# A four-layer graph network: PSUM handed out by single banks, rows turned by transposing transfers, parts of elu and beta added by transfers, and a new order of the work

## The chip, the cores and the metric

The kernel runs on one core of one Trainium2 chip. A core has five instruction queues that run side by side: TensorE (PE), VectorE (DVE), ScalarE (ACT), GpSimd (POOL) and SyncE (SP). Each takes its instructions strictly in the order in which the program lists them, and waits at one whose data or buffer is not there. Matmul results go to PSUM, which has eight banks of 512 float32 columns; the other tiles lie in SBUF. The metric is the time of one execution on the device in microseconds; less is better.

## The reference

There are eight graphs of 2048 nodes with 128 features in float32, and one 2048 x 2048 matrix of edges for all of them. Each of four layers normalizes the rows (layer norm, then the larger of the value and 0), works on the result `h`, and adds what comes out to `x`:

```
layers 0, 1, 3:  Wh = h W;  e = leaky_relu(Wh a1 + (Wh a2)^T);  no edge: -9e15
                 x += f(softmax(e) Wh)        f: elu, nothing, elu
layer 3:         Wh is normalized first, and added to softmax(e) Wh before elu
layer 2:         four heads of 32 features:  e = leaky_relu(h h^T);  no edge: -inf
                 x += softmax(e) h
```

## The kernel before, in words

**Units.** A graph's layer is a unit: 24 graph units (class `Gat`, layers 0, 1 and 3) and 8 of heads (class `Heads`, layer 2). Within a graph its layers follow one another; the eight graphs are independent, and the kernel mixes units of different graphs.

**Building a unit.** VectorE takes the moments of the rows (L471), POOL the power -1/2 (L113), ScalarE makes the rows `h` in four quarters of 512 nodes (L538). A quarter is turned, so that the features lie on the partitions: four 128 x 128 transposes on TensorE into PSUM (L569), then a copy to SBUF. For a graph unit ScalarE copies it to `h_t` (L590), TensorE multiplies it with the weights (L599), and ScalarE makes from the products the values `y` and the exponentials of the scores (L637 to L652). For heads the copy (L964) rounds it to `hi`, VectorE takes the rest `lo` (L968), and SP stores both parts and `h` to DRAM (L973, L952), from where they are loaded again head by head: `s` (L987), `m` (L995), `v` (L1000).

**Tokens.** A graph unit's attention goes by two halves of 1024 target nodes and 16 blocks of source nodes; a half and a block is a token, 768 in all. VectorE makes the 128 x 1024 weights `zg` with one instruction (L767), and TensorE adds eight 128 x 129 products to three PSUM banks (L776; in float32 each shows as two matmuls). After 16 tokens VectorE divides by the sums into `oa` (L808, L809). Layer 1 adds `oa` to `x` by an accumulating transfer that POOL issues (L845). Layers 0 and 3 apply elu, with -1 taken beforehand: ScalarE makes exp of `oa` into `oe` and the larger of `oa` and 0 (L815), VectorE adds the smaller of `oe` and 1 to `x` (L839), and a transfer adds `oa`. Layer 3 first adds the rows by a transfer (L893), multiplies by gamma (L832) and adds beta (L834) on VectorE. There is one `oa` and one `oe`. The last graph's layer 3 and a few places listed in `DIRECT` use VectorE instead of transfers.

**Beats.** A head and a block of 128 source nodes is a beat, 512 in all. TensorE makes 128 x 2048 scores with four matmuls in two pairs (L1063), ScalarE takes exp of each pair's 1024 columns (L1070), VectorE masks all 2048 columns with one instruction that also adds them up (L1076), and TensorE multiplies with the values in 32-column tiles (L1085). After a head's 16 beats the result is copied, turned, divided and added to `x` by a transfer (L1094 to L1110).

**PSUM.** Banks 1 to 3 hold a token half's sums and bank 0 a head's result. Banks 4 to 7 are two pairs, taken by whatever else needs PSUM: scores, transposes, projections, small sums.

**Who sets the order.** `Plan` (L178) is a planner that runs when the program is built. Each piece of work is added with its engine, a cost, a due time, what it needs, and the buffers it takes and frees (L191); `run` (L201) then starts, step by step, on the engine that can start first, the piece of lowest due time among those ready within a small window. The order found is each queue's order in the program. The slots of each buffer stand in L262. Due times come from three tables: `TOKENS` (start of each half), `BEATS` (start and step of each head) and `LEADS` (how long before its start a unit is begun).

## Time and profile before

| what | value |
|---|---|
| runs | 2681.71 us median of 3 (2679.57 to 2682.79) |
| profiled execution | 2679.22 us, its span 2677.4 us, granted TensorE clock 0.992 |
| first and last score matmul | 280.6 us, 2542.6 us |
| TensorE idle time | 78.8 us in all, 34.4 of it between 268 and 2546 us |
| tokens on VectorE (L767) | 768 of 1.279 us |
| masks on VectorE (L1076) | 512 of 2.285 us |
| exps on ScalarE (L1070) | 1024 of 1.111 us |
| VectorE adds of 128 x 1024 (L834, L839) | 16 of 1.220 us, 32 of 1.221 us |
| accumulating transfers of 512 KB (L845, L893) | 40 and 14; POOL busy 0.9 us each; 4.9 and 4.6 us to landing |
| bytes moved | 196.49 MB, 73 GB/s on average |

A line of the profile's groups names the source line, engine and operation, what is written and read, and how often; behind the bar stand the busy time in us, the mean of one in ns, and the idle time of the engine just before them, with what ended most of it. PEld is TensorE's loading of weights, which runs beside matmuls. Overlapping instructions count once in a busy time, so that a mean can be larger than busy time over count.

### The profile page before, as it was taken

The numbers are of one execution on the slowest core, as the hardware profiler recorded it, in microseconds if no ns is written. First come the engines' busy times: TensorE is split into PE (matmuls) and PEld (weight loads), VectorE is DVE, ScalarE is ACT, GpSimd is POOL, SyncE is SP. The second block draws the span as 40 slices with busy tenths as digits, with TensorE's granted clock in tenths as the row PEclk, the third lists the DMA queues.
The fourth block names the chain that finished last, engine by engine and source line by source line (L and its number), as shares of the span: only waits on it lengthen the run. The fifth ranks groups of instructions, "written<-read, shape, count | busy, mean of one in ns | idle before, by whom it ended". The sixth has DMA issues, their size and how long they took to land. (4 is left out here: it accounts for less than half of the span.)

```text
span 2677.4 us, 49161 instructions
## 1 busy us (share of the span) xinstructions
PE 2598.6 (97%) x20104; PEld 2041.9 (76%) x20104; DVE 2482.8 (93%) x3304; ACT 1719.8 (64%) x2777; POOL 279.8 (10%) x143
## 2 busy tenths in 40 slices
PE   7999999999999999999999999999999799999997
PEld 7899877687777786888777768787766478676587
DVE  8867989989999999999999999999999799999987
ACT  2526555767776677647766778674676866778751
POOL 1200000010100110011110101011101110010020
PEclk9999999999999999999999999999999999999999
DMA  9002423144344332362424434424315321542121
GB/s 319 17 9 63 97 52 67 10 94 103 81 88 99 62 62 56 60 123 56 86 50 87 79 78 87 82 48 88 72 42 93 64 40 56 115 68 64 33 52 34
DMA packets 216875, 196.49 MB, mean 73 GB/s; under 512 B 142896, under 2 KB 178176, under 8 KB 210496
## 3 DMA queue, kind: packets, MB, share of 16 engines
q1 hardware_dynamic: 144112, 156.46, 22.5%
q0 software_dynamic: 72112, 36.73, 12.0%
q8 instruction: 160, 2.62, 0.4%
q14 instruction: 75, 0.61, 0.1%
q10 hardware_dynamic: 416, 0.07, 0.0%
HBM read 123.03 MB, written 33.73 MB: 59 GB/s over the span
## 5 line engine op out<-in xcount | busy, mean ns | idle before, releaser
L776 PEld LDWEIGHTS ps<-y,zg 128*128 128x128 f32 x12288 | 1449.5, 192 | 66.1 <-DVE zg L767 17.0
L776 PE MATMUL ps<-y,zg 128*128 128x129 f32 x12288 | 1472.5, 276 | 13.6 <-DVE zg L767 10.0
L1070 ACT ACTIVATE z<-ps,shift 128x1024 f32<-128x1024 f32 x1024 | 1091.1, 1111 | 525.4 <-PE ps L1063 513.4
L1076 DVE SCALAR_TENSOR_TENSOR z<-z,edge 128x2048 f32<-128x2048 f32 x512 | 1160.0, 2285 | 26.9 <-ACT z L1070 26.6
L767 DVE SCALAR_TENSOR_TENSOR zg<-r,cr,edge 128x1024 f32<-128x1024 f32 x768 | 969.4, 1279 | 113.6 <-PE ps L776 101.9
L1063 PE MATMUL ps<-m,s 128*128 128x512 f32 x2048 | 627.0, 421 | 21.8 <-ACT z L1070 10.9
L1063 PEld LDWEIGHTS ps<-m,s 128*128 128x128 f32 x2048 | 341.0, 190 | 268.4 <-ACT z L1070 147.8
L1085 PE MATMUL ps<-z,v 128*32 128x512 f32 x4096 | 499.7, 601 | 1.5 <-DVE z L1076 1.3
L1085 PEld LDWEIGHTS ps<-z,v 128*32 128x32 f32 x4096 | 103.9, 109 | 223.8 <-issue 175.0
L538 ACT ACTIVATE h<-x,nmrx,rstdx 128x128 f32<-128x128 f32 x512 | 207.0, 485 | 48.5 <-DVE nmrx L118 36.0
L113 POOL TENSOR_TENSOR rstdx<-varx,neg_half 128x16 f32<-128x16 f32 x31 | 122.1, 3940 | 458.0 <-DVE varx L108 444.6
L1110 POOL DMA_DIRECT2D x<-o x31 | 65.8, 2124 | 747.9 <-DVE o L1105 608.2
L845 POOL DMA_DIRECT2D x<-oa x40 | 36.9, 922 | 748.5 <-ACT z L1070 199.5
L599 PE MATMUL ps<-rhs,h_t 128*128 128x130 f32 x768 | 104.9, 283 | 4.6 <-DVE h_t L590 2.7
L599 PEld LDWEIGHTS ps<-rhs,h_t 128*128 128x128 f32 x768 | 95.4, 195 | 12.6 <-ACT h_t L590 7.1
L471 DVE BATCH_NORM_STATS2 st<-x 128x6 f32<-128x128 f32 x496 | 100.4, 278 | 3.3 <-DMA x<-oa 3.3
L569 PE MATMUL ps<-ident,h 128*128 128x128 f32 x512 | 79.7, 280 | 4.2 <-ACT z L1070 1.7
L809 DVE TENSOR_TENSOR oa<-ps,rs 128x384 f32<-128x384 f32 x144 | 73.9, 513 | 5.1
L815 ACT ACTIVATE oe<-oa 128x1024 f32<-128x1024 f32 x32 | 33.9, 1058 | 69.0 <-DVE oa L834 55.3
L590 ACT COPY h_t<-ps 128x512 f32<-128x512 f32 x92 | 52.6, 585 | 33.2 <-PE ps L569 33.1
L569 PEld LDWEIGHTS ps<-ident,h 128*128 128x128 f32 x512 | 60.9, 143 | 16.6 <-ACT h L538 4.3
L637 ACT ACTIVATE y<-ps,y 128x128 f32<-128x128 f32 x240 | 68.6, 369 | 0.0
(129 smaller groups left out, 833.8 us busy)
## 6 DMA issues: line engine op xcount, KB each, us to landing
s<-halves SPq DMA_DIRECT2D x256, 128.0 KB, 2.8
m<-halves SPq DMA_DIRECT2D x64, 512.0 KB, 6.8
r<-row SPq DMA_DIRECT2D x42, 512.0 KB, 3.9
x<-oa POOLq DMA_DIRECT2D x40, 512.0 KB, 4.9
raw<-in_adj_dram SPq DMA_DIRECT2D x16, 1024.0 KB, 15.5
values<-h SPq DMA_DIRECT2D x32, 256.0 KB, 2.3
halves<-hi SPq DMA_DIRECT2D x128, 64.0 KB, 1.7
halves<-lo SPq DMA_DIRECT2D x128, 64.0 KB, 1.7
```

The source lines that it names most:

```text
L113: nc.gpsimd.tensor_tensor(out=rstd, in0=v, in1=neg_half, op=OP.pow)
L471: nc.vector.bn_stats(out=key["st"][:, n, :], in_=rows()[:, n, :])
L538: nc.scalar.activation(self.h[q][:, k, :], X[self.b][:, n, :], AF.Relu, scale=key["rstd"][:, n:n + 1], bias=key["nmr"][:, n:n + 1])
L569: nc.tensor.transpose(pk[:, k, :], self.h[q][:, k, :], ident)
L599: nc.tensor.matmul(pv[:, k, :C + 2], lhsT=self.h_t[q][:, k * P:(k + 1) * P], rhs=rhs, start=True, stop=True)
L767: nc.vector.scalar_tensor_tensor(z, self.r[half], self.cr[:, 0, jb:jb + 1], edge[:, jb, half * HN:(half + 1) * HN], op0=OP.max, op1=OP.mult)
L776: nc.tensor.matmul(ps[:, self.banks(half, place)[i // 3], k * CE:(k + 1) * CE], lhsT=z[:, i * P:(i + 1) * P], rhs=self.y[:, jb, :], start= ...
L809: nc.vector.tensor_mul(key["a"][:, i0:i1, :], pv[:, :, :C], r[:, i0:i1, None].to_broadcast([P, i1 - i0, C]))
L1063: nc.tensor.matmul(ps[:, lo + c, :], lhsT=self.S[h, jb // HB][:, at:at + P], rhs=self.M[h][:, (c2 * 2 + c) * 512:(c2 * 2 + c + 1) * 512], ...
L1070: nc.scalar.activation(self.z[s][:, c2 * HN:(c2 + 1) * HN], ps[:, lo:lo + 2, :].rearrange("p b t -> p (b t)"), AF.Exp, bias=shift)
L1076: nc.vector.scalar_tensor_tensor(self.z[s], self.z[s], 1.0, edge[:, jb, :], op0=OP.mult, op1=OP.mult, accum_out=self.den[:, h, jb:jb + 1])
L1085: nc.tensor.matmul(ps[c * HD:(c + 1) * HD, 0, :], lhsT=self.V[h][:, jb, :], rhs=z[:, c * 512:(c + 1) * 512], start=jb == 0, stop=jb == NB - 1,
```

## The change

*Single banks.* The planner hands out banks 4 to 7 one by one. A work item can take two of them (the second place for a half's sums). Each score matmul and each exp of 512 columns is an item of its own; projections, the values made of them, and the exponentials that TensorE spreads over all partitions for three units are split by bank.

*Rows turned by transfers.* In all units but the seven in `ON_PE`, ScalarE copies a quarter's low and high 16 bits into two planes `pl`, SP issues one transposing transfer of `pl` to `tr`, and ScalarE merges the planes into `h_t`. `pl` and `tr` have one buffer each; `h` has two instead of three. For heads, `hi` and `lo` are then made from `h_t` in SBUF, and `lo` overwrites it.

*Parts of elu and beta by transfers.* ScalarE makes the larger of -`oa` and 0, then exp of its negative, which is the smaller of exp(`oa`) and 1, so that a transfer can add it to `x`; three ScalarE instructions instead of two. In graphs 0 to 6, beta is added to `oa` by a transfer from a source that is repeated. The last graph and `DIRECT` keep VectorE's add of elu.

*Order.* The costs and delays that the planner reckons with are others; token halves follow a list `HALVES` at a fixed distance, heads start at `PLACES`, and `LEADS` is new. 

```diff
-        plan = Plan(dict(pair=(4, 6), sums=(0,), more=(1,), low=0, z=5, zg=3, r=2, h=3, h_t=2, hi=1, lo=1,
+        plan = Plan(dict(bank=(4, 5, 6, 7), sums=(0,), more=(1,), low=0, z=5, zg=3, r=2, h=2, h_t=2, pl=1, tr=1, hi=1,
...
+    PLANES, TURNED, ON_PE = 1, 1, ((0, 0), (1, 0), (0, 1), (0, 2), (7, 1), (7, 2), (7, 3))
...
+            def turned_by_transfer(self, q, part, made, kept=None):
+                key = {}
+                def split(op):
+                    key["pl"] = big.tile([P, 2, 4 * P], U16, tag="pl", name="pl", bufs=PLANES)
+                    nc.scalar.copy(key["pl"], self.h[q].rearrange("p k c -> p (k c)").bitcast(U16).rearrange(
+                        "p (n two) -> p two n", two=2))
+                def move(op):
+                    key["tr"] = big.tile([P, 8, P], U16, tag="tr", name="tr", bufs=TURNED)
+                    nc.sync.dma_start_transpose(out=key["tr"], in_=key["pl"].rearrange("p two n -> p (two n)"))
+                def merge(op):
+                    self.h_t[q] = quarter("h_t")
+                    nc.scalar.copy(self.h_t[q].bitcast(U16).rearrange("p (n two) -> p two n", two=2),
+                                   key["tr"].rearrange("p (two k) n -> p two (k n)", two=2))
+                parted = add("ACT", SPLIT_US, self.due(part), split, made[1:], takes=["pl"], frees=[] if kept else [("h", made[0])])
+                moved = add("SP", MOVE_US, self.due(part), move, [parted, kept], takes=["tr"],
+                            frees=[("pl", parted)] + [("h", made[0])] * (kept is not None),
+                            lag=MOVE_LAG_US)
+                return add("ACT", MERGE_US, self.due(part), merge, [moved], takes=["h_t"], frees=[("tr", moved)])
...
-                    turn = self.transposes(q, part, made[q], ["h_t"])
+                    by_pe = (self.b, layer) in ON_PE
+                    turn = self.transposes(q, part, made[q], ["h_t"]) if by_pe else None
...
+                        copied = turn = self.turned_by_transfer(q, part, made[q])
...
+                def below(op):
+                    key["e"] = key.get("e") or big.tile([P, HB, C], F32, tag="oe", name="oe", bufs=1)
+                    nc.scalar.activation(key["e"], key["a"], AF.Relu, scale=-1.0)
+                def grown(op):
+                    nc.scalar.activation(key["e"], key["e"], AF.Exp, scale=-1.0)
...
-                    e = e_taker = add("ACT", 0.95, due + 6, lambda op: whole(op, "e", AF.Exp), [last], takes=["oe"])
+                    e_taker = add("ACT", 0.95, due + 6, below, [last], takes=["oe"])
+                    e = add("ACT", 0.95, due + 7, grown, [e_taker])
...
+                        if k == 2 and b != B - 1:
+                            last = add("POOL", PLUS_US, due + 6 + 4 * k, lambda op: nc.gpsimd.dma_start(
+                                out=key["a"], in_=beta2_sb[:, None, :].to_broadcast([P, HB, C]), accum_op=OP.add),
+                                [last], lag=PLUS_LAG_US)
...
-                e = add("DVE", 1.14, late, elu_e, [e], frees=[("oe", e_taker)])
+                if (b, layer) in DIRECT or b == B - 1:
+                    e = add("DVE", 1.14, late, elu_e, [e], frees=[("oe", e_taker)])
+                else:
+                    e = add("POOL", PLUS_US, late, lambda op: nc.gpsimd.dma_start(
+                        out=xs(), in_=key["e"], accum_op=OP.add), [e], frees=[("oe", e_taker)], lag=PLUS_LAG_US)
...
+                        nc.scalar.copy(self.h_t[q, 0], rows_t(q, turn, by_pe))
...
+                        self.h_t[q, 1] = (quarter("h_t") if by_pe else self.h_t[q]).bitcast(F32R)
+                        nc.vector.tensor_sub(self.h_t[q, 1], rows_t(q, turn, by_pe), self.h_t[q, 0].bitcast(F32))
...
-                        for c2 in range(2):
-                            score = add("PE", 0.463, due - EARLY["score"] + c2, lambda op, s=s, c2=c2: self.scores(op, s, c2),
-                                        [score, ops[jb // HB], ops[2]], takes=["pair"] + ["z"] * (c2 == 0))
+                        for c in range(4):
+                            score = add("PE", SCORE_US, due - EARLY["score"] + 0.5 * c, lambda op, s=s, c=c: self.scores(op, s, c),
+                                        [score, ops[jb // HB], ops[2]], takes=["bank"] + ["z"] * (c == 0), lag=0.28)
...
+            def exp(self, op, s, c, bank):
+                if c == 0:
                     self.z[s] = big.tile([P, N], F32, tag="z", name="z", bufs=5)
+                nc.scalar.activation(self.z[s][:, c * 512:(c + 1) * 512], ps[:, bank, :], AF.Exp, bias=shift)
...
+        HALVES = (
+            (1, 0, 0), (1, 0, 1), (0, 1, 0), (0, 1, 1), (2, 0, 0), (2, 0, 1), (1, 1, 0), (1, 1, 1),
...
+        PLACES = (
+            374.047, 498.948, 515.464, 607.589, 669.983, 722.264, 807.407, 892.766, 873.536, 927.774,
...
```

## The prediction

> **What bounds the kernel now.** First the totals of the busy time, then the costliest groups of instructions.
>
> ```profile
> PE 2598.6 (97%) x20104; PEld 2041.9 (76%) x20104; DVE 2482.8 (93%) x3304; ACT 1719.8 (64%) x2777; POOL 279.8 (10%) x143
> ...
> L1070 ACT ACTIVATE z<-ps,shift 128x1024 f32<-128x1024 f32 x1024 | 1091.1, 1111 | 525.4 <-PE ps L1063 513.4
> L1076 DVE SCALAR_TENSOR_TENSOR z<-z,edge 128x2048 f32<-128x2048 f32 x512 | 1160.0, 2285 | 26.9 <-ACT z L1070 26.6
> L767 DVE SCALAR_TENSOR_TENSOR zg<-r,cr,edge 128x1024 f32<-128x1024 f32 x768 | 969.4, 1279 | 113.6 <-PE ps L776 101.9
> L569 PE MATMUL ps<-ident,h 128*128 128x128 f32 x512 | 79.7, 280 | 4.2 <-ACT z L1070 1.7
> L590 ACT COPY h_t<-ps 128x512 f32<-128x512 f32 x92 | 52.6, 585 | 33.2 <-PE ps L569 33.1
> ```
>
> TensorE is idle for 78.8 of 2677.4 us. ScalarE stands 513.4 us waiting for scores and VectorE 101.9 us for room that TensorE frees: both wait for TensorE. A busy TensorE need not be at its pace, so next I read the order in time of the weight loads, where starts follow one another if nothing is waited for.
>
> ```profile
> 1265.74 1.98 PEld L776 LDWEIGHTS ps<-y,zg 128*128 128x128 f32 x16
> 1267.63 0.47 PEld L569 LDWEIGHTS ps<-ident,h 128*128 128x128 f32 x4
> 1268.07 0.30 PEld L1063 LDWEIGHTS ps<-m,s 128*128 128x128 f32 x2
> 1268.42 3.77 PEld L776 LDWEIGHTS ps<-y,zg 128*128 128x128 f32 x32
> 1272.11 0.47 PEld L569 LDWEIGHTS ps<-ident,h 128*128 128x128 f32 x4
> 1272.55 0.30 PEld L1063 LDWEIGHTS ps<-m,s 128*128 128x128 f32 x2
> ```
>
> No waits stand here. Start to start, a token (16 loads, L776) after scores takes 1.89 us (1265.74 to 1267.63); two in a row take 3.69, so the second 1.79 or so. A quarter's four transposes (L569) take 0.44, both times. So removing them moves all that follows up by 0.44.
>
> Third, three stretches: from the start to the first scores, the middle in which heads and tokens are mixed, and the last tokens.
>
> ```profile
> 0.00:268.00 268.00, 244.77 (x2067) 234.57 (x2068) 202.97 (x357) 111.94 (x325) 32.30 (x25) 0.97 0.31 102
> 268.00:2546.00 2278.00, 2243.57 (x17072) 1699.55 (x17071) 2173.04 (x2793) 1561.97 (x2345) 233.41 (x111) 1.00 0.36 72
> 2546.00:2677.40 131.40, 110.22 (x970) 107.77 (x968) 106.83 (x155) 45.88 (x108) 14.13 (x8) 0.96 0.21 44
> ```
>
> Columns: window and length, then busy us of PE, PEld, DVE, ACT, POOL, clock, DMA share, GB/s. In the middle TensorE is 98.5% busy, VectorE 95.4%, ScalarE 69%: TensorE bounds, VectorE is close behind. Of the middle's 34.4 us without TensorE, 14.8 lie in one place:
>
> ```profile
> 2077.00:2144.00 67.00, 52.16 (x316) 29.27 (x319) 48.17 (x64) 54.08 (x105) 7.92 (x3) 0.92 0.33 63
> ```
>
> There ScalarE makes a unit's rows while the exps wait behind them in its order. The list of waits over the span (us in total, times, longest) has what follows from that:
>
> ```profile
> DVE z L1076 <- ACT z L1070: 26.6, 19, 16.9
> ...
> PE ps L1063 <- ACT z L1070: 10.9, 12, 3.3
> ```
>
> The longest wait of the first line, 16.9 us, stands in that window: VectorE has no exp to mask. So ScalarE's order can cost time even at 64%. The last line is TensorE's wait for a score bank that ScalarE has not emptied.
>
> **The change, part by part.** *Transposes.* 25 of 32 units (all but the seven in ON_PE) turn rows by transfer: 100 quarters. TensorE loses 100 x 0.44 = 44.0 us, on the path. Added per quarter: a split (128x1024 two-byte elements) and a merge on ScalarE, one transfer on SP. A graph unit's quarter loses a copy of 0.585. The nearest row of ScalarE for the split is the copy of 128x1024 floats, 1.007 us; I take 1.0 each, with ends 0.585 (half the bytes, L590) and 2.0 (128x2048, L442). ScalarE: 100 x 2.0 - 76 x 0.585 = +156 us (73 to 356). It is hidden as long as the exps behind it aren't late: ScalarE now stands 513 us waiting for scores.
>
> *The transfer's landing* is shown nowhere in this trace. Nearest rows, both 256 KB:
>
> ```profile
> values<-h SPq DMA_DIRECT2D x32, 256.0 KB, 2.3
> x<-o POOLq DMA_DIRECT2D x31, 256.0 KB, 7.8
> ```
>
> The first moves whole rows, the second adds in pieces of 128 bytes. I take 4, nearer the first, since the source rows are whole. A merge that ScalarE reaches before the landing blocks all exps queued behind it. In the changed program's order I summed ScalarE's own work between each split and its merge, with durations from the rows above and exps at 0.535: 2.1 to 20 us, median 6.4. Standing at the merges, over all 100, is then at most 0.2 us at a landing of 2.3, 11 at 4, 48 at 6, 149 at 7.8. I take 11, which the 513 us absorb: 0 on the path. SP carries 100 more issues; it stands before loads of s for 718.8 us over 46 waits (38.7 at most), so a transfer queued behind such a load starts late by that; the order interleaves them, and my 11 doesn't hold it: the upper end does. With one buffer each for pl and tr a unit's four quarters take at least 4 x (1.0 + 4 + 1.0) = 24 us, 39 at a landing of 7.8; that is hidden where a unit is begun early, and where one is not (the unit built from 2085 to 2116 took 31) up to some 10 us are late: rival (c). h has two buffers instead of three, but gives one back at the split or the transfer; the lo part is subtracted from SBUF instead of PSUM (0.685, taken as the same).
>
> By the Trainium skill's page "VectorE: DVE Perf Modes" (Rules for kernel authors, with The three transpose paths) TensorE should turn 128x128 blocks where PSUM will do; it has 1309 ns per block by transfer, and the eight two-byte blocks of a quarter would land after 10.5 us, an estimate. Then the standing would be 377 us and the change a loss if a seventh of it reached TensorE. The row of 256 KB above, 2.3 us, speaks for less, and no row here shows a transposing transfer.
>
> A second rule speaks against my bound: the skill's start page, "Trainium Kernel Development and Optimization" (Best Practices), judges TensorE by the share of its weight loads, not by its busy time. That is 76% here, and by it the 44 us would buy little. The starts 0.44 us apart with no wait between say otherwise.
>
> *Single banks.* Each score matmul takes its own bank and each exp has 512 columns: 2048 exps at 0.585 less the 0.05 by which neighbours overlap (1.111 against a start distance of 1.06) make 1096 against 1091: +5 us of ScalarE; without the overlap 1198, +107. A bank comes free after half the time, so I take the 10.9 us wait of TensorE as gone (0 to 34.4, the middle's idle time). Counted in both programs, changes between scores and tokens rise from 664 to 691; a token after scores starts its successor 0.10 later than one after a token, so +2.7 us. Projections go from one product of 8 loads to two of 4: same loads.
>
> *elu and beta.* VectorE loses 26 of L839 (1.221) and 14 of L834 (1.220): 48.8 us. ScalarE gains 32 x 1.058 = 34. POOL issues 40 more adds at 0.9 = 36 us, and the one that adds a waits for the landing of the one that adds e (4.9). Queued behind on POOL are powers (3.9 each) and gathers; VectorE waited only 5.2 us for powers. The single oa of a layer-3 half is held about 29 us instead of 19, of a layer-0 half 17 instead of 11; a half takes at least 16 x 1.79 = 28.6 us of TensorE, 55 on average, so the next divide is not late. Were it late, VectorE and the sums' three banks would stand, at most about 10 us per half. Value 0 on the path, as VectorE is not the pace.
>
> *Order.* In the changed program 127 tokens stand before the first score instead of 105, 56 after the last score in both. The front grows by 22 x 1.79 = 39.4 us and the middle shrinks by as much. VectorE in the middle then needs 2173.0 - 22 x 1.26 - 48.8 = 2096 of 2278.0 - 39.4 - 44.0 + 2.7 - 10.9 = 2186 us, 95.9% as against 95.4%: its relief is used up by the order, TensorE stays ahead. ScalarE in the middle: 1562 + 156 + 34 + 5 = 1757, 80%. Other stalls I leave as they are: a new order has other ones.
>
> Sum against the profiled execution (span 2677.4 + 1.8 = 2679.2): -44.0 + 2.7 - 10.9 = 2627.0. That execution lay 2.5 below the median of the runs shown, so 2629.5; I say 2630.
>
> **Rivals.** (a) *Slower: ScalarE stands at the merges.* One mechanism at the merge line. With 52.2 us to give back, it decides where the standing that reaches TensorE passes 52: from a landing of 6.2 us if all reaches it, 9.2 if a fifth does. At 7.8 and two thirds reaching: +99, 2730. For it: 2077 to 2144, and ten merges with under 4 us of work before them. Against: 513 us of slack at the exps, five z buffers, the 2.3 row.
> (b) *The gain is larger.* If the new order also loses the 14.8 us hole and the rest of the middle's idle time (23.5 beyond my 10.9): about 2606; half of the 44 idle outside the middle too: 2584.
> (c) *Most is given back* on ScalarE at 80% in the middle: 156 us more in the builds of 25 units, of which a fifth surfaces: 2661.
> (d) *No change*: the transposes stood where VectorE was the pace. VectorE's 95.4% in the middle speaks for some of that, but it too is relieved.
>
> **How the numbers follow.** The likeliest, 0.55, gives 2630 with its own range 2608 to 2655 (nothing of the 10.9, or all of the middle's idle time, and a dozen us of new stalls). (b) 0.17, (c) 0.10, (d) 0.04, (a) 0.14. The range 2585 to 2690 leaves out the far end of (b) and most of (a). About 0.2% (5 us) is what a measurement can tell from no change. Faster 0.82, same 0.04, slower 0.14.
>
> **What would show it.** Right: 112 transposes on TensorE at about 17 us instead of 79.7, TensorE's busy time near 2553 at 97% of the span, VectorE near 2434, ScalarE near 1910, transfers landing under 5 us, no large wait of ScalarE for the tile tr. Wrong: ScalarE waits for tr in the tens of us, the wait of VectorE for exps far above 26.6, TensorE's share falling to 95%, split or merge near 2 us, or POOL's queue making powers late so that rows wait.

## The result and the profile after

The changed kernel takes 2681.53 us (median of 20 runs, 2675.87 to 2686.98), the kernel before, run beside it, 2680.82 us (20 runs, 2678.69 to 2682.79). The ratio is 1.0000, with a 95% interval of 0.9994 to 1.0007: no change, where 2630 was forecast. The profiled execution took 2684.46 us, its span 2682.6 us at a granted clock of 0.989. Two runs in a slower state of the chip, one of the kernel before at 3290.02 us and one of experiment 6 at 3763.16 us, are left out of the times below.

First the page's totals and costliest groups of the changed kernel, in the columns already known.

```profile
PE 2594.0 (97%) x19704; PEld 2008.5 (75%) x19704; DVE 2443.3 (91%) x3268; ACT 2073.6 (77%) x4218; POOL 318.0 (12%) x183
...
L1129 ACT ACTIVATE z<-ps,shift 128x512 f32<-128x512 f32 x2048 | 1246.8, 710 | 238.0 <-PE ps L1123 237.0
L1134 DVE SCALAR_TENSOR_TENSOR z<-z,edge 128x2048 f32<-128x2048 f32 x512 | 1162.3, 2284 | 52.7 <-ACT z L1129 51.8
L802 DVE SCALAR_TENSOR_TENSOR zg<-r,cr,edge 128x1024 f32<-128x1024 f32 x768 | 968.3, 1279 | 115.0 <-PE ps L811 97.6
...
L579 ACT COPY h_t<-tr 128x1024 uint16<-128x1024 uint16 x100 | 137.1, 1371 | 38.1 <-DMA tr<-pl 26.8
...
L570 ACT COPY pl<-h 128x1024 uint16<-128x1024 uint16 x100 | 105.6, 1056 | 0.7
```

ScalarE is busy 2073.6 us instead of 1719.8. The exps (L1129) account for 155.7 of the 353.8 (1246.8 against 1091.1), the splits (L570) and merges (L579) for 242.7, less the copies that they replace. TensorE has 400 instructions fewer, and its busy time is only 4.6 us less. The same kernel's groups show the transposes that are left, and its list of transfers what the turning ones take from issue to landing.

```profile
L593 PE MATMUL ps<-ident,h 128*128 128x128 f32 x112 | 17.4, 291 | 0.0
```

```profile
oa<-beta_sb POOLq DMA_DIRECT2D x14, 512.0 KB, 6.6
tr<-pl SPq DMA_TRANSPOSE x100, 3.3
```

The transposes went from 79.7 to 17.4 us, and the transfers land after 3.3 us. So the change did what it says. Next the list of waits of the changed kernel (us in total, times, longest).

```profile
ACT z L1129 <- PE ps L1123: 237.0, 248, 15.9
PEld ps L1123 <- ACT z L1129: 184.8, 304, 1.8
...
DVE zg L802 <- PE ps L811: 97.6, 134, 6.7
...
DVE z L1134 <- ACT z L1129: 51.8, 52, 7.0
...
ACT h_t L579 <- DMA tr<-pl: 26.8, 16, 4.3
```

The second of these lines read so before:

```profile
PEld ps L1063 <- ACT z L1070: 147.8, 172, 3.8
```

ScalarE waits for scores 237 us instead of 513; TensorE's weight loads wait for banks that ScalarE empties 184.8 us, 304 times, instead of 147.8 us, 172 times; VectorE's masks wait for exps 51.8 us instead of 26.6. The last line of the list above, the wait at the merges, is small and never over 4.3 us. Last, two tables by stretches (columns as before: window and length, busy us of PE, PEld, DVE, ACT and POOL, clock, DMA share, GB/s), the first by stages.

```profile
0.00:300.00 300.00, 274.62 (x2397) 266.50 (x2398) 232.47 (x410) 138.61 (x419) 39.54 (x30) 0.98 0.37 109
300.00:2538.00 2238.00, 2203.43 (x16331) 1629.59 (x16331) 2106.45 (x2709) 1887.06 (x3679) 260.79 (x142) 0.99 0.49 91
2538.00:2682.60 144.60, 116.00 (x980) 112.36 (x979) 104.33 (x151) 47.91 (x120) 17.70 (x11) 0.92 0.27 47
```

```profile
268.00:335.00 67.00, 61.36 (x474) 54.65 (x473) 49.12 (x52) 35.64 (x87) 2.98 (x3) 0.95 0.67 143
...
1407.00:1474.00 67.00, 60.99 (x441) 45.93 (x444) 52.44 (x50) 51.79 (x113) 5.53 (x5) 0.95 0.69 133
...
2077.00:2144.00 67.00, 66.83 (x508) 48.88 (x510) 66.48 (x86) 57.28 (x136) 10.23 (x6) 1.00 0.45 79
```

In the middle TensorE is busy 2203.43 of 2238 us, 98.5%, to the tenth the share of before. The hole at 2077 is gone (66.83 of 67.00 us busy), but others have come, such as the one at 1407 with 60.99 (the others of 67 us begin at 268, 1005, 1742 and 2412, with 61.4 to 63.7).

**Where the 44 us went.** A busy share cannot tell, so I counted from the starts of TensorE's matmuls. For each pair of neighbouring kinds of work (a token after scores, scores after sums, and so on), the tenth percentile of the distance between their starts, over twelve of the kernels of this study, is taken as that pair's time without a wait. The sum of these is TensorE's work, and what the real distances have beyond it are its stalls. This is an own reckoning, good to some us. In us:

| kernel | work | stalls | of these before scores | before tokens | before projections |
|---|---|---|---|---|---|
| before | 2488 | 170 | 94 | 27 | 9 |
| changed | 2439 | 222 | 109 | 58 | 21 |

TensorE's work fell by 49 us, a little more than the forecast's 44.0. Its stalls rose by 52. The "97% busy" of before hid 170 us in which TensorE's instructions followed one another late; most of that counts as busy. The clock explains little of the 52: the profile has TensorE's granted clock at half for 13.7 us of the middle before and for 27.9 us of it in the changed kernel, which is at most 7 us of lost pace.

### The profile page after: what moved, and what is told of

It reads as the page before. It is cut to its first block, busy times and chain, and to the rows that moved or that the text cites. A ratio compares the mean times of both kernels' runs of the same rounds, so it can differ in the third digit from the quotient of the medians.

```text
span 2682.6 us, 50019 instructions
## 1 busy us (share of the span) xinstructions
PE 2594.0 (97%) x19704; PEld 2008.5 (75%) x19704; DVE 2443.3 (91%) x3268; ACT 2073.6 (77%) x4218; POOL 318.0 (12%) x183
## 3 DMA queue, kind: packets, MB, share of 16 engines
q0 software_dynamic: 90416, 57.70, 17.4%
## 5 line engine op out<-in xcount | busy, mean ns | idle before, releaser
L1129 ACT ACTIVATE z<-ps,shift 128x512 f32<-128x512 f32 x2048 | 1246.8, 710 | 238.0 <-PE ps L1123 237.0
L1134 DVE SCALAR_TENSOR_TENSOR z<-z,edge 128x2048 f32<-128x2048 f32 x512 | 1162.3, 2284 | 52.7 <-ACT z L1129 51.8
L1123 PE MATMUL ps<-m,s 128*128 128x512 f32 x2048 | 663.1, 430 | 16.7 <-ACT z L1129 4.8
L1123 PEld LDWEIGHTS ps<-m,s 128*128 128x128 f32 x2048 | 347.2, 189 | 303.8 <-ACT z L1129 184.8
L538 ACT ACTIVATE h<-x,nmrx,rstdx 128x128 f32<-128x128 f32 x512 | 209.4, 493 | 34.9 <-DVE nmrx L119 27.3
L114 POOL TENSOR_TENSOR rstdx<-varx,neg_half 128x16 f32<-128x16 f32 x31 | 114.5, 3694 | 576.6 <-DVE varx L109 503.2
L579 ACT COPY h_t<-tr 128x1024 uint16<-128x1024 uint16 x100 | 137.1, 1371 | 38.1 <-DMA tr<-pl 26.8
L570 ACT COPY pl<-h 128x1024 uint16<-128x1024 uint16 x100 | 105.6, 1056 | 0.7
L974 POOL DMA_DIRECT2D x<-oe x26 | 23.2, 894 | 501.4 <-ACT oe L857 501.4
L667 ACT ACTIVATE y<-ps,y 128x128 f32<-128x128 f32 x240 | 75.3, 365 | 0.0
```

What stands on the lines that cost most here:

```text
L114: nc.gpsimd.tensor_tensor(out=rstd, in0=v, in1=neg_half, op=OP.pow)
L538: nc.scalar.activation(self.h[q][:, k, :], X[self.b][:, n, :], AF.Relu, scale=key["rstd"][:, n:n + 1], bias=key["nmr"][:, n:n + 1])
L570: nc.scalar.copy(key["pl"], self.h[q].rearrange("p k c -> p (k c)").bitcast(U16).rearrange("p (n two) -> p two n", two=2))
L579: nc.scalar.copy(self.h_t[q].bitcast(U16).rearrange("p (n two) -> p two n", two=2), key["tr"].rearrange("p (two k) n -> p two (k n)", two=2))
L1123: nc.tensor.matmul(ps[:, op.got["bank"], :], lhsT=self.S[h, jb // HB][:, at:at + P], rhs=self.M[h][:, c * 512:(c + 1) * 512], start=True, ...
L1129: nc.scalar.activation(self.z[s][:, c * 512:(c + 1) * 512], ps[:, bank, :], AF.Exp, bias=shift)
```

## The experiments

Three theories at the outset. A: TensorE's pace sets the time, so 44 us did come out, and something put them back. B: they hardly came out at all, because TensorE's busy time holds stalls that widen when work is taken away. C: ScalarE's added work put them back. Other rivals are described in the text that names them.

**1 and 2. One relief at a time, in the kernel before.** Its own order is kept.

```diff
-                    for k in range(4):
+                    for k in range(1):
                         nc.tensor.transpose(pk[:, k, :], self.h[q][:, k, :], ident)
```

> The kernel before with its own order, but only the first of each quarter's four transposes; the copies read that one block four times, so the output is not the reference's. TensorE loses 128 x 3 x 0.11 = 42 us of start-to-start time, nothing else changes. Theory A (the prediction's: TensorE is the pace of the kernel before): 2639, 35 to 44 us less. Theory B (TensorE's busy time hides stalls, 170 us by the starts of its matmuls, and the pace is set by the chain of scores, exps and masks through three queues): less than half of it comes out, 5 to 20 us less.

Measured: 2669.03 us, ratio 0.9954 (0.9938 to 0.9971), 12 us less. By my count TensorE's work fell 41 us and its stalls rose from 170 to 201. The number is B's: of 42 us taken from TensorE some 30 turned into waiting. The chain that B names as the cause is not shown by it.

The other half of the change's relief, VectorE's adds:

```diff
-    nc.vector.scalar_tensor_tensor(xs(), key["e"], 1.0, xs(), op0=OP.min, op1=OP.add)
+    n = HB if b == B - 1 or (b, layer) in DIRECT else 1
+    nc.vector.scalar_tensor_tensor(xs()[:, :n, :], key["e"][:, :n, :], 1.0, xs()[:, :n, :], op0=OP.min, op1=OP.add)
```

> The kernel before with its own order, but the 40 VectorE adds that the change gives to transfers (26 of elu, 14 of beta) cover one eighth of their columns, so elu and beta are left out for the rest. VectorE loses about 40 x 1.0 = 40 us, nothing else changes. If VectorE is the pace in the middle: 30 to 40 us less. Theory A: 0 to 5 less. Theory B: 5 to 20 less.

Measured: 2680.4 us, 0.9998 (0.9988 to 1.0007). VectorE's busy time fell from 2482.8 to 2450.5 us and the time did not move. As forecast, VectorE is not the pace.

**3, 4, 9 and 10. ScalarE's additions taken out of the changed kernel**, in its own order. The exps take fewer columns (384, later 436), or the splits and merges an eighth of theirs.

```diff
-    nc.scalar.activation(self.z[s][:, c * 512:(c + 1) * 512], ps[:, bank, :], AF.Exp, bias=shift)
+    nc.scalar.activation(self.z[s][:, c * 512:c * 512 + 384], ps[:, bank, :384], AF.Exp, bias=shift)
```

> The changed kernel with its own order, but each exp covers 384 of its 512 columns (the rest of the scores keeps what an earlier head left there). ScalarE loses about 2048 x 0.107 = 219 us, against 156 us that cutting the exps in two had added; no other engine loses work. Theory C (ScalarE's added 354 us made exps and values late and gave the 44 us back): 2625 to 2645. Rival D (the new order has its stalls whatever ScalarE's load is): 2670 to 2682.

> The changed kernel with its own order, but all splits after the first and all merges handle an eighth of their elements (the rest of the turned rows keeps what was there before). ScalarE loses about 100 x (0.8 + 1.05) = 185 us, the transfers and all waits stay. Theory C: 2630 to 2655. Rival D: 2670 to 2682. If it is the waits for the transfers themselves: 2675 or more.

> The changed kernel in its own order, with each exp taking 436 of its 512 columns (the other columns of the weights keep what was there, so the output is not the reference's): two exps then cost what one exp of 1024 columns cost before, about 1.01 to 1.02 us, where two of 512 are 1.14 us apart, and ScalarE's exps lose some 115 to 130 us, about what halving the exps had added. Theory C (ScalarE's added work gave the gain back; the exps' half of it and the split's and merge's half each cost about 20 us): 2655 to 2662 us, in line between 2681 with 512 columns and 2644 with 384. Rival (the cost of an exp has a knee, and all of the 37 us at 384 columns came from the load below that of the kernel before): within 5 us of the changed kernel, 2676 to 2684.

> The same with the splits and merges at an eighth of their columns too (the turned rows of all but the first such quarters are left over from it, so the output is not the reference's): ScalarE's work is back near that of the kernel before, and TensorE still has its 400 transposes fewer. Theory C: the two halves add to what the prediction's sum had, 2630 to 2645 us (2681 less 20 for the splits and merges, less 20 to 25 for the exps). Rival (the new order itself, not ScalarE's load, keeps TensorE waiting): 2655 or more, little below either edit alone.

| edit in the changed kernel | us | ratio to before | ScalarE busy | TensorE's stalls |
|---|---|---|---|---|
| none | 2681.53 | 1.0000 (0.9994 to 1.0007) | 2073.6 | 222 |
| splits and merges short | 2661.17 | 0.9921 (0.9904 to 0.9937) | 1904.5 | 200 |
| exps of 436 columns | 2650.17 | 0.9876 (0.9859 to 0.9892) | 1949.0 | 190 |
| exps of 384 columns | 2643.94 | 0.9861 (0.9845 to 0.9878) | 1870.3 | 182 |
| 436 columns, and splits and merges short | 2640.95 | 0.9853 (0.9836 to 0.9869) | 1784.1 | 177 |

Both halves of ScalarE's addition cost time: 20 us for the splits and merges, 31 for what the exps cost beyond those of before. Together they give 41, less than their sum. TensorE's work is the same in all five; only the stalls change. With ScalarE's additions out, TensorE waits about as long as before (177 against 170), and 41 of the 49 us of saved work show in the time. The waits of the last row:

```profile
PEld ps L1141 <- ACT z L1147: 133.8, 180, 1.5
...
DVE z L1152 <- ACT z L1147: 27.3, 29, 5.9
```

TensorE's loads wait 133.8 us for banks, 180 times (184.8 and 304 in the changed kernel, 147.8 and 172 before), and VectorE's wait for exps is back at 27.3 us (26.6 before). This is the state in which the forecast thought the changed kernel would run.

**11 to 14. The same cuts in the kernel before: a control.**

```diff
-    nc.scalar.activation(self.z[s][:, c2 * HN:(c2 + 1) * HN],
-                         ps[:, lo:lo + 2, :].rearrange("p b t -> p (b t)"), AF.Exp, bias=shift)
+    nc.scalar.activation(self.z[s][:, c2 * HN:c2 * HN + 768],
+                         ps[:, lo:lo + 2, :].rearrange("p b t -> p (b t)")[:, :768], AF.Exp, bias=shift)
```

> The kernel before in its own order, with each exp taking 768 of its 1024 columns (the other columns of the weights keep what was there, so the output is not the reference's): ScalarE's 1024 exps lose about 0.2 us each, some 200 us, as much as three quarters of the columns saved in the changed kernel. Theory C (ScalarE decides only where its load is high, as in the changed kernel, and at the load of before it has slack): 2668 to 2682, at most a third of the 37 us that the same cut gave there. Rival (exps stand in TensorE's way in either kernel, and the cut helps as much wherever it is made; then the changed kernel's gain was not given back by ScalarE's added work): 2640 to 2655.

Measured: 2680.69 us, 0.9999 (0.9989 to 1.0008). The cut that gave the changed kernel 37 us gives nothing here. In the kernel before, with ScalarE at 64%, its exps stand in nobody's way; the gains above belong to the changed kernel.

> The kernel before in its own order with both cuts: exps of 768 of 1024 columns and one of a quarter's four transposes (both leave work out, so the output is not the reference's). This is as near as the old order comes to TensorE losing 42 us with ScalarE out of the way; the transposes alone gave 12 us. Theory C with ScalarE as what follows TensorE: the transposes give more here than alone, 2635 to 2655. Rival (the old order was fitted to TensorE's old work, and VectorE's chain of masks and gates is next in line): 2656 to 2670, no more than the two cuts' own gains added.

> The kernel before in its own order, with one of a quarter's four transposes (TensorE 42 us less; alone it gave 12) and the 40 moved additions of VectorE at an eighth of their columns (VectorE 40 us less; alone it gave nothing). Reading 1 (in the old order VectorE is close behind TensorE, so the missing 30 us of the transposes come once VectorE falls too): 2635 to 2655. Reading 2 (the old order itself, with its places fitted to the old TensorE work, holds the rest, and VectorE does not matter): 2662 to 2670, no further than the transposes alone.

> The same with exps of 768 of 1024 columns too (each of the three leaves work out, so the output is not the reference's): TensorE, VectorE and ScalarE all lose at least what the change takes from TensorE and VectorE, in the old order. With the two cuts of TensorE and ScalarE it was 2665. Reading 1: 2632 to 2650. Reading 2: 2658 to 2666; the changed kernel with ScalarE's additions taken out reached 2641, so 20 us of that would then belong to the new order and not to the engines' work.

Measured: 2665.15 us, 0.9948 (0.9931 to 0.9965), with exps and transposes cut; 2665.09, 0.9946 (0.9930 to 0.9963), with adds and transposes; 2663.46, 0.9940 (0.9924 to 0.9957), with all three. So 16, 15 and 17 of TensorE's 42 us. I had leaned to more in each; neither ScalarE's nor VectorE's load holds the rest. In the last one TensorE's work is 2447 us and its stalls are 195, 25 more than before, most of them before projections (16 instead of 9), before tokens (32 instead of 27) and before groups of sums (13 instead of 7). The old order itself does not pass on what TensorE saves. The changed kernel with ScalarE's additions taken out reached 2640.95, 22 us below the last of these, although ScalarE has more to do there (1784.1 us against 1502.3). Some 8 us of that are work that TensorE saves there and not here (49 us against 41); the rest belongs to the new order and its single banks.

**5 and 6. Adding work to ScalarE in the kernel before**, in its own order: each exp as two of 512 columns, and then the rows of the 25 units made twice.

```diff
-    nc.scalar.activation(self.z[s][:, c2 * HN:(c2 + 1) * HN],
-                         ps[:, lo:lo + 2, :].rearrange("p b t -> p (b t)"), AF.Exp, bias=shift)
+    for k in range(2):
+        at = c2 * HN + k * 512
+        nc.scalar.activation(self.z[s][:, at:at + 512], ps[:, lo + k, :], AF.Exp, bias=shift)
```

> The kernel before with its own order and pairs of banks, but each exp of 1024 columns is issued as two of 512, one after the other. ScalarE gains 1024 x (2 x 0.570 - 1.013) = 130 us (the distances of back-to-back exps in the two profiles); nothing else changes and the output is the reference's. Theory C (ScalarE's work costs time although it is idle a third of the span; the two cuts in the changed kernel gave 0.11 and 0.17 us per us): 2695 to 2703. Rival D (in the kernel before ScalarE's idle time covers it, only the new order is sensitive): 2679 to 2686.

Measured: 2684.33 us, 1.0012 (1.0002 to 1.0022). The group of exps is now like the changed kernel's:

```profile
L1072 ACT ACTIVATE z<-ps,shift 128x512 f32<-128x512 f32 x2048 | 1242.5, 690 | 388.0 <-PE ps L1063 387.3
```

ScalarE has 151 us more of exps, and the time rose by 2.6. At the load and in the order of before the halved exps are as good as free, as the prediction's sum had it.

```diff
-                    for k in range(4):
+                    twice = (self.b, self.layer) not in ((0, 0), (1, 0), (0, 1), (0, 2), (7, 1), (7, 2), (7, 3))
+                    for k in [0, 1, 2, 3] * (1 + twice):
```

> The kernel before with its own order, but the rows of the 25 units that the change turns by transfers are made twice by ScalarE: about 100 x 1.5 = 150 us more of ScalarE, at the place where units are built, no other work and no wait added; the output is the reference's. Theory C: 2698 to 2708. Rival D: 2679 to 2686. If work in the builds is worse than work at the exps, because the exps wait behind it: above 2708.

Measured: 2804.95 us, 1.0456 (1.0434 to 1.0479): 123 us more for some 152 us of ScalarE. Its waits:

```profile
ACT z L1071 <- PE ps L1064: 518.0, 424, 10.5
...
DVE zg L768 <- PE ps L777: 164.9, 152, 7.2
...
DVE z L1077 <- ACT z L1071: 49.2, 27, 22.3
```

ScalarE still stands 518 us waiting for scores. The 513 us that the forecast took for slack were no reserve for work in another place: work that the order did not reckon with in a unit's build cost 0.8 us for each us, while exps halved between their neighbours, with which it did not reckon either, cost next to nothing. Two things go into the 0.8. TensorE's own loads for the transposes and projections of the builds stood 102.6 us instead of 29.2. And the granted clock of the span fell from 0.992 to 0.980, some 35 us of lost pace. What such work costs where the planner has reckoned with it, as with the splits and merges, this run does not show; the 20 us above do.

**7, 8, 15 and 16. Orders planned anew.** The changed kernel with all transposes on TensorE, and with pairs of banks again, the tables of due times as they were:

```diff
-    PLANES, TURNED, ON_PE = 1, 1, ((0, 0), (1, 0), (0, 1), (0, 2), (7, 1), (7, 2), (7, 3))
+    PLANES, TURNED, ON_PE = 1, 1, tuple((b, n) for b in range(8) for n in range(4))
```

> The changed kernel with all units in ON_PE: no transposing transfers, splits and merges; the order is planned anew with the same tables. TensorE gains 44 us, ScalarE loses 198. Theory C: 22 to 34 us less by ScalarE, some 13 more by TensorE (12 of 42 came out when it was taken away): 2660 to 2675, if the new order is no worse. If the transfers were a gain by themselves: 2690 to 2725.

```diff
-                        for c in range(4):
+                        for c in range(2):
...
-                                        [score, ops[jb // HB], ops[2]], takes=["bank"] + ["z"] * (c == 0), lag=0.28)
+                                        [score, ops[jb // HB], ops[2]], takes=["bank"] * 2 + ["z"] * (c == 0), lag=0.28)
```

> The changed kernel with scores and exps by two banks again (any two of the four; 1024 exps of 1024 columns, booked at 1.013), the planner's window at 0.12 instead of 0.148, and the order planned anew with the same tables. ScalarE loses 130 us, TensorE's and VectorE's work stays. Theory C: 2660 to 2668 if the order is as good; the tables were made for single banks, so up to 2690. If single banks are a gain that outweighs their 130 us: above 2690.

Measured: 2784.13 us, 1.0383 (1.0365 to 1.0402), and 2839.86 us, 1.0594 (1.0576 to 1.0613). Both missed by 100 us and more. They tell little of transposes and banks: with other costs or buffers the planner makes another order out of the same tables, and that order is measured along with the edit. So I searched new tables, with costs of ScalarE's work as the trace has them.

```diff
-    SPLIT_US, MOVE_US, MOVE_LAG_US, MERGE_US = 0.94, 1.28, 4.5, 1.207
+    SPLIT_US, MOVE_US, MOVE_LAG_US, MERGE_US = 1.0, 1.25, 2.2, 1.31
...
-                            exps.append(add("ACT", 0.51, due - EARLY["exp"] + 0.5 * c, lambda op, s=s, c=c, sc=score: self.exp(
+                            exps.append(add("ACT", 0.57, due - EARLY["exp"] + 0.5 * c, lambda op, s=s, c=c, sc=score: self.exp(
```

> The changed kernel's whole computation, with an order searched anew for ScalarE's costs as the trace has them: an exp of 512 columns booked at 0.57 us instead of 0.51, a split at 1.0 and a merge at 1.31 instead of 0.94 and 1.207, a turning transfer at 3.45 in all instead of 5.78, the values y at 0.79 instead of 0.71 (0.5 instead of 0.3 in layer 3). One more unit (graph 6, layer 3) turns on TensorE. Theory C (TensorE's 44 us were given back where ScalarE's work falls due later than the order assumed): the order can step round part of it, 2645 to 2668, faster than both kernels; 2641, which the changed kernel reached with ScalarE's additions taken out, is about the floor. Rival (the order was as good as it gets at that load of ScalarE): 2675 to 2700.

> The same, with PSUM handed out in pairs as in the kernel before: exps of 1024 columns at 1.013 us, whose work on ScalarE is about 130 us less than that of two of 512, and 22 instead of 25 units turning rows by transfers; the order searched for that. Theory C with ScalarE's exps as half of what was given back: 2640 to 2665, at or below the kernel with single banks. Rival (a pair of banks holds scores back more than the shorter exps cost): 2670 to 2700, above it.

Measured: 2711.9 us, 1.0107 (1.0087 to 1.0127), and 2782.77 us, 1.0382 (1.0365 to 1.0400). Both are misses again: I had expected 2640 to 2668. The first at least is far better than the orders planned without a search, but the changed kernel's own order is 30 us better, although it reckons with an exp of 0.51 us. That ScalarE's costs were booked too low is therefore not shown to be what the order lacks. One thing does tell the two kernels with pairs apart from those with single banks: TensorE's matmuls of scores wait for exps 82.9 and 70.0 us in them (experiments 8 and 16), 7.7 and 20.5 us in the others (7 and 15), and 4.8 us in the changed kernel. In the kernel before, whose order was made for pairs, it was 10.9.

**17 and 18. Fewer, longer exps in the changed kernel's own order.** After the planning, two neighbouring exps become one of 1024 columns at the second one's place, where the first one's bank is not handed on in between (954 of 1024 pairs).

```diff
+        for s1, e1, s2, e2 in halves_of:
+            a, b = s1.got["bank"], s2.got["bank"]
+            if not any(a in op.all.get("bank", ()) for op in plan.order[at[id(e1)] + 1:at[id(e2)]]):
+                joined[id(e1)], joined[id(e2)] = None, (min(a, b), max(a, b))
```

> The changed kernel in its own order, planned for single banks, but wherever two neighbouring exps of a beat read two banks of which the first is not handed on before the second exp's place (about nine in ten of the 1024 pairs), they become one exp of 1024 columns at the second one's place, over the two banks wherever they lie. The whole computation is done. ScalarE's exps lose some 115 us (two of 512 columns are 1.14 us apart, one of 1024 1.01), as with 436 columns; the first half's exp starts about 0.57 us later and its bank is held that much longer. Theory C: the order with measured gain at 436 columns (2650) less what the later banks cost, 2650 to 2668, faster than both kernels. Rival (the banks held longer stop scores, as with pairs before): 2675 to 2700.

Measured: 2792.82 us, 1.0413 (1.0399 to 1.0427), 111 us more instead of 15 to 30 less. ScalarE is busy 1949.2 us, within 0.2 of the kernel with exps of 436 columns, which took 2650. So ScalarE's load cannot be all; the timeline shows what else. First the changed kernel (start us, length us, engine, line, instructions, and in brackets what was waited for):

```profile
1202.04 0.75 PEld L1123 LDWEIGHTS ps<-m,s 128*128 128x128 f32 x4 [0.84 <-ACT z L1129]
1202.04 1.19 PE L1123 MATMUL ps<-m,s 128*128 128x512 f32 x4
1202.57 2.42 ACT L1129 ACTIVATE z<-ps,shift 128x512 f32<-128x512 f32 x4 [0.56 <-PE ps L1123]
...
1202.84 1.98 PEld L811 LDWEIGHTS ps<-y,zg 128*128 128x128 f32 x16
```

Then the kernel with joined exps:

```profile
1204.87 0.53 PEld L1129 LDWEIGHTS ps<-m,s 128*128 128x128 f32 x3 [0.84 <-ACT z L1140]
...
1205.64 1.11 ACT L1140 ACTIVATE z<-ps,shift 128x1024 f32<-128x1024 f32 x1 [0.79 <-PE ps L1129]
...
1206.80 0.19 PEld L1129 LDWEIGHTS ps<-m,s 128*128 128x128 f32 x1 [1.40 <-ACT z L1140]
1206.81 0.50 PE L1129 MATMUL ps<-m,s 128*128 128x512 f32 x1 [0.97 <-ACT z L1140]
1206.91 1.99 PEld L812 LDWEIGHTS ps<-y,zg 128*128 128x128 f32 x16
```

With single banks four scores run through, and the next token's loads start 0.80 us after the first score's (1202.04 to 1202.84). With joined exps three scores run, the fourth stands 1.40 us for a bank, and the token behind it starts 2.04 us after the first (1204.87 to 1206.91). Over the span the waits of TensorE's loads for exps grew from 184.8 to 276.8 us, and those of its matmuls from 4.8 to 86.9 (partly the same time):

```profile
PEld ps L1129 <- ACT z L1140: 276.8, 363, 2.1
...
PE ps L1129 <- ACT z L1140: 86.9, 156, 1.9
```

The halved exps thus are the price of this order's way of handing out banks, and joining them in it costs more than they do. It also means that the 31 us of exps at 436 columns may in part be banks that come free earlier, not load alone; these runs don't part the two. The 20 us of the splits and merges, where the exps stay as they are, can't come from shorter exps.

> The same, with the 100 splits of turned rows made by GpSimd, at the same place of the order, which stands idle 88% of the span. ScalarE loses another 106 us. Theory C: 2640 to 2658, some 10 us below the joined exps alone. Rival (GpSimd's queue, where powers and accumulating transfers stand waiting some 500 us each, or a slow copy there, makes the turned rows late): 2670 to 2720, slower than the joined exps alone.

```diff
-                    nc.scalar.copy(key["pl"], self.h[q].rearrange("p k c -> p (k c)").bitcast(U16).rearrange(
+                    nc.gpsimd.tensor_copy(key["pl"], self.h[q].rearrange("p k c -> p (k c)").bitcast(U16).rearrange(
```

Measured: 2811.17 us, 1.0482 (1.0468 to 1.0497), 18 us above the run before it. A split takes 1.737 us on GpSimd, where it took 1.046 on ScalarE in the run before it, and GpSimd stands 215 us in all at the splits, until a transfer has read `pl` and frees it. No version faster than both kernels was found among those that compute everything.

## Why the prediction was wrong, point by point

The step that failed is the fourth point below: ScalarE's additions, put at 0 on the path, cost 41 us.

- *"Removing them moves all that follows up by 0.44."* This holds in the new order and not in the old. The distance is real, and TensorE's work fell by 49 us. In the changed kernel 41 us of that show in the time once ScalarE's additions are out. In the kernel before's order only 12 of 42 us came out, 17 with ScalarE and VectorE relieved too: I read one undisturbed stretch of weight loads and put its pace on the whole middle, in which 115 us of stalls lay inside a busy share of 98.5%. That the new order would have no more stalls than the old (177 against 170 without ScalarE's additions) was assumed and not worked out; that it came so is luck. The rule that I set aside, of the Trainium skill's start page, "Trainium Kernel Development and Optimization" (Best Practices), that matmul busy time is no measure of the distance to roofline (the hardware's limit), agrees with the stalls found here. That by it the 44 us would buy little was my own inference, and it holds for the old order alone.
- *Exps "+5 us of ScalarE".* Mis-sized: +155.7 us busy, beyond my upper end of 107, so that ScalarE gained 354 us in all and not the 195 of my sum (156 + 34 + 5). I had taken the duration of a copy of 128 x 512 for an exp of that shape. Two exps of 512 columns start 0.57 us apart (1.14 for 1024), one of 1024 columns takes 1.01: halving adds about 0.13 us each time.
- *Splits and merges, 1.0 us each.* The split was right (1.056), the merge was 1.371. The wait at the merges was 26.8 us instead of 11, small as forecast; the landing 3.3 us instead of 4. Rival (a) is out: no merge waited over 4.3 us. The Trainium skill's page "VectorE: DVE Perf Modes" (The three transpose paths) has 1309 ns for a block; the 10.5 us for eight blocks that I had worked out from it as an estimate are not what one transfer of eight takes here, 3.3 us.
- *"Which the 513 us absorb: 0 on the path"*, and ScalarE's other additions at 0 with it. This is the step that failed, and it gave the gain back. Of the 513 us 237 are left, and each addition cost time: 20 us for splits and merges, 31 for the exps, 41 for both (2681.53 against 2640.95). A total of waits is no reserve; what counts is whether there is room at the place and in the moment, as the 152 us at the builds of the kernel before showed (+123) beside the 151 us of halved exps (+2.6). By which route the exps' part reaches TensorE, by load or by banks that come free later, stays open.
- *Rival (c)*, most is given back on ScalarE, was right in kind, with a chance of 0.10 and at 2661 too small: ScalarE in the middle stood at 84% (1887 of 2238 us), not 80, and all of the gain was given back.
- *Rival (d)*, no change because VectorE was the pace, had the number and not the cause: VectorE relieved alone gave nothing (2680.4 us), and with the transposes no more than they gave alone, within the noise (ratio 0.9946 against 0.9954). That 2681.53 lies between my ends of 2585 and 2690 is luck too: that part of the range stood for (a) and small new stalls.
- *The bank wait of 10.9 us gone, changes of work +2.7.* TensorE's work, which holds the changes, fell by 49 instead of 41.3; the wait of 10.9 went to 4.8, but that of the weight loads for banks rose from 147.8 to 184.8. The joined exps show how much an order that was planned for single banks hangs on them (111 us and more). What single banks are worth beside pairs with an order made for pairs, no run shows cleanly.
- *elu and beta at 0 on the path*: right as far as tested. VectorE's busy time fell by 39.5 us (48.8 forecast), and relieving it alone moved nothing. POOL rose by 38.2 us (36). ScalarE's share, three instructions of 1.07 to 1.09 us instead of two, was as forecast.
- *"Other stalls I leave as they are."* The hole at 2077 went, five others came. A new order can't be costed from the old one's holes.

What stays open besides: why the old order keeps 25 of TensorE's 42 us even with the two other engines relieved, and whether the new order with its transposes put back in place would be slower than 2681. The one try at it planned another order and doesn't answer.

## What to carry to other kernels

Before pricing work removed from a busy engine, count its stalls from the starts of its instructions: a share of 97% hid 170 us here, and 42 us taken out in the old order gave 12. Price what the change adds to other engines with a row of the same operation, not of another one of the same shape, and ask if there is room at the place where it lands, not in the engine's total of waits. In a kernel whose order is fixed when it is built, an edit that keeps the order is the easier experiment to read; four that planned it anew came out 30 to 158 us above the changed kernel, whatever they were to show.

## What was unexpected of the hardware

- A transposing transfer of 256 KB of two-byte elements takes 3.3 us from issue to landing, nearer to a plain transfer of that size (2.7 us, values to DRAM) than to an accumulating one (8.2 us for 256 KB into `x`).
- The same 128 x 1024 two-byte elements take ScalarE 1.056 us to split into planes and 1.371 us to merge from them.
- Splits on GpSimd made VectorE's own instructions longer, though the work was the same. The groups of the kernel with joined exps, and then of that with the splits on GpSimd:

```profile
L803 DVE SCALAR_TENSOR_TENSOR zg<-r,cr,edge 128x1024 f32<-128x1024 f32 x768 | 969.9, 1279 | 152.8 <-PE ps L812 133.7
```

```profile
L803 DVE SCALAR_TENSOR_TENSOR zg<-r,cr,edge 128x1024 f32<-128x1024 f32 x768 | 1005.8, 1326 | 127.9 <-PE ps L812 111.0
```

A token's instruction of 1.279 us takes 1.326 in the mean, a mask 2.322 instead of 2.285, and VectorE is busy 64 us more (2514.4 against 2450.0), for 174 us of copies on GpSimd.
